# One layer of attention and experts: no long step in the second round, two adding transfers to a round

## The chip, the core and the metric

The kernel runs on one core of a Trainium2 chip. The core has five engines, each with a queue of its own that is worked off in order: TensorE (PE; its weight loads are listed apart as PEld), VectorE (DVE), ScalarE (ACT), GpSimd (POOL) and SyncE (SP, which issues DMAs). 16 DMA engines move data between the device's memory, called DRAM here, and the on-chip buffers. The metric is the device time of one execution in microseconds (us), lower is better.

## What is computed

The input x is [32, 256, 128] in float32: 32 sequences of 256 tokens with 128 features. Cut to what matters:

```python
xn = layernorm(x)
# attention: 16 heads of 8, rotary positions, a window of 64 tokens, causal
q, k, v = split(xn @ Wqkv.T); q, k = rotate(q), rotate(k)
a = softmax(where(allow, q @ k.T / sqrt(8), -inf)) @ v
attn = a @ Wproj.T + bproj
# experts: 8, of which each token takes 2
weights, indices = top_k(xn @ gate_w.T + gate_b, 2); weights = softmax(weights)
ffn = sum over e of w_e * (gelu(xn @ w1[e] + b1[e]) @ w2[e] + b2[e])
out = x + attn + ffn
```

## The kernel before

**Units of work.** Attention goes sequence by sequence (z = 0 to 31). Norms, projections and the tiles xs[u] (the input in SBUF, to which all results are added) go by pairs of sequences (u = 0 to 15). Routing goes by groups of 16 token tiles (g = 0 to 3, four u each).

**Rounds.** The order of the work on every engine is written out by hand. `Attention.run` goes through four rounds r for each sequence. A round emits the scores `sh` (L689, L701) of sequence z, of which DVE takes the maxima (L715), and the scores `sl` (L756, L770) of an earlier sequence, which ACT exponentiates (L780). `sh` has one buffer in PSUM, so the next round's `sh` can't begin before L715 is through. Besides, round 0 has the values of sequence z - 2 (L792, L801) and in odd z the sum of the rotated k (L618); round 1 the projection of the next pair (L596 on PE, L605 and L612 on DVE, then the rotation's product L611 on POOL); round 2 the second half of the values and the division (L801 to L827); round 3 in odd z the sum of the rotated q, then `parts` (L726 to L729) and `end` of sequence z - 2, which projects the attention's result and adds it into one half of xs[u] (L841, on DVE). `alone` (L627) copies the rotated k and q into the layouts km (in round 1, for the next sequence) and qm (in round 2) by four DMAs each on SP's queue.

**Beside the rounds.** At the end of each round `turn` takes one step of a second strand of work, `beside`, and then emits what was put off for POOL, among it L611:

```python
def turn(z, r):
    self.now = z, r
    next(beside, None)
    self.flush()
```

In this strand come, one after the other: norms and routing with the scatters; the experts; the collecting.

- *Norms and routing.* `norm` (L277) yields True before a long step (two tiles of L286 and L287 on DVE; the second one also has L289) and False before a light one (ACT's normalizing L303, PE's transposes L310 and gates L315, and so on). `route` (L326) does the same, with long steps on DVE of two to four instructions. In each round every strand that waits at a light step takes it; of long steps as many are taken as `room` says for that round (L1229).
- *Scatters.* Once a group is routed, its tokens are written to DRAM in the order of their experts (xs_d, L502), 128 indirect DMAs on POOL's queue, two to a round.
- *Experts.* When all scatters are issued, the loads of the first four blocks are issued, two more rounds pass, and then all 78 blocks of the experts are emitted in one round (L1011 to L1119). They write their results to ys_d in DRAM (L1087), one row for each token and choice.
- *Collecting.* `collect` (L1122) goes over the 16 u twice, for the first and the second choice (k = 0 and 1). One adding transfer (L1128, issued by POOL) reads 256 KB of ys_d and adds it to xs[u] in SBUF. After the second one of a u, those of its two sequences whose `end` is done are written to the output by `out` (L849, on SP's queue); the others are written by `end`. One transfer is issued to each `yield`, so to each round.

All accesses to xs[u] are kept in program order: `end` waits for an adding transfer into its xs[u] that was emitted before it, a transfer for an `end` before it, an output for both.

Of the kernel before, what the change touches and what calls it, by code (L numbers as in the profile page):

```python
# [105 lines left out]
def tile_layer(  # L106
# [87 lines left out]
    def loads_late():  # L194
        for u in range(3, NU):
            yield False
            load_x(u)
            if u == 3:
                nc.sync.dma_start(out=b1_n, in_=b1)
# [319 lines left out]
    class Attention:  # L519
# [327 lines left out]
        def out(self, z):  # L847
# [4 lines left out]
            )  # L852

        def run(self, beside):
            us = self.us
            first, stop = 2 * us[0], 2 * us[-1] + 2
# [15 lines left out]
# [4 lines that stand above are left out]
                self.past.clear()  # L876
# [245 lines left out]
    def collect():  # L1122

        for k in range(2):
            for u in range(NU):
                yield
                at = k * B * T + u * TB
                nc.gpsimd.dma_start(  # L1128
                    out=xs[u], in_=ys_d[at : at + TB, :].rearrange("(n p) d -> p n d", p=P),
                    accum_op=ALU.add,  # L1130
                )
                if k:
                    att.added.add(u)
                    for z in (2 * u, 2 * u + 1):
                        if z in att.ended:
                            att.out(z)

    def beside():
# [11 lines left out]
        def pack():  # L1150

            for e in range(NE):
                yield False
                nc.sync.dma_start(out=w_d[e, :, 0:H], in_=w1[e])
                nc.sync.dma_start(
                    out=w_d[e, :, H : H + NHC * D].rearrange("p (k d) -> p k d", d=D),
                    in_=w2[e].rearrange("(k p) d -> p k d", p=P),
                )
                yield False
                nc.sync.dma_start(  # L1160
                    out=w_d[e, :, H + NHC * D :], in_=b2_d[e : e + 1, :].to_broadcast([P, D])
                )

        def fills():

            yield False
            fill(0, NE)
            for e in range(NE):
                end = nc.sync.value_load(
                    ends[0:1, e : e + 1], min_val=ER * e, max_val=ER * (e + 1) - HT  # L1170
                )
                spread.append(
                    nc.sync.dma_start(
                        out=xs_d[bass.ds(end, HT), :], in_=void[:, e]
                    )
                )
                if e % 2:
                    yield False
# [21 lines left out]
        def begin(name, steps, urgent=False):  # L1200
            entry = [name, steps, next(steps)]
            going.insert(0, entry) if urgent else going.append(entry)

        def go_on(entry):
            entry[2] = next(entry[1], None)
            if entry[2] is None:
                finished.add(entry[0])
                going.remove(entry)
# [10 lines left out]
        u, g, last = 2, 0, False  # L1219
        while next(transfers, transfers) is not transfers:  # L1220
            z, r = att.now
            if (z, r) == (1, 0):
                begin("loads", loads_late())
            if (z, r) == (1, 1):
                begin("masks1", att.masks(1))
            if (z, r) == (3, 0):
                begin("pack", pack())

            room = ((2, 2, 0, 0) if z == 0 else (1, 1, 0, 1) if z % 2 else (2, 1, 0, 1))[r]  # L1229
            light = [e for e in going if e[2] is False]  # L1230
            for entry in light:
                go_on(entry)
            while room > 0:
                due = [e for e in going if e[2] is True and e not in light]
                if due:
                    go_on(due[0])
                elif u < NU:
                    begin(f"norm{u}", norm(u))
                    u += 1
                    continue  # L1240
                else:
                    break
                room -= 1
            if g < NG and all(f"norm{n}" in finished for n in range(NU // NG * (g + 1))):
                begin(f"route{g}", route(g, rt, misc), urgent=True)
                g += 1
            slots.extend(n for n in range(NG) if f"route{n}" in finished and n not in slots)
            if len(slots) == NG and not last:
                begin("blocks", blocks(rt, misc))
                last = True  # L1250
            if "blocks" in finished and "fills" not in [e[0] for e in going] + list(finished):
                begin("fills", fills())
            yield
# [3 lines left out]
        yield from experts()  # L1257
        apart(returned, "returned")
        yield from collect()

    att.run(beside())
    pools.close()

# [32 lines left out]
```

## Time and profile before

| | |
|---|---|
| median of 7 runs | 768.41 us (761.46 to 782.73) |
| the profiled execution | 757.22 us, span 755.4 us, granted TensorE clock 0.995 |
| busy: PE, DVE, POOL, ACT | 708.0, 494.7, 400.7, 385.2 us |
| L715, the maxima on DVE | 128 x 1220 ns |
| L780, the exponentials on ACT | 128 x 1023 ns |
| L502, scatters, on POOL | 128 x 993 ns |
| L1087, results of the experts, on POOL | 135 x 957 ns |
| from the start of L715 of round 1.0 to that of 22.3 | 29.09 to 350.28 us |
| round 22.3, with the experts | 350.28 to 616.85 us |
| rounds 23.0 to the end | 616.85 to 755.4 us |

A round z.r is round r of sequence z. The page of a profile gives the busy time of each engine over the span; "busy" doesn't say that an engine is what the others wait for. So the span is cut at the starts of L715, which comes once a round, and the windows between are compared with one another: a sequence with nothing beside it shows what attention alone takes. A timeline's row has start, duration, engine, line, tiles, count, and in brackets the idle time before it with what ended it.

### The profile page before, as it was taken

The numbers are of one execution on the slowest core, as the hardware profiler recorded it, in microseconds if no ns is written. First come the engines' busy times: TensorE is split into PE (matmuls) and PEld (weight loads), VectorE is DVE, ScalarE is ACT, GpSimd is POOL, SyncE is SP. The second block draws the span as 40 slices with busy tenths as digits, with TensorE's granted clock in tenths as the row PEclk, the third lists the DMA queues.
The fourth block names the chain that finished last, engine by engine and source line by source line (L and its number), as shares of the span: only waits on it lengthen the run. The fifth ranks groups of instructions, "written<-read, shape, count | busy, mean of one in ns | idle before, by whom it ended". The sixth has DMA issues, their size and how long they took to land.

```text
span 755.4 us, 20155 instructions
## 1 busy us (share of the span) xinstructions
PE 708.0 (94%) x7579; PEld 461.4 (61%) x7579; DVE 494.7 (65%) x1203; ACT 385.2 (51%) x727; POOL 400.7 (53%) x653
## 2 busy tenths in 40 slices
PE   7999999998999998998999999999999999999896
PEld 3445545444544444444999999899899964444342
DVE  5688998988998898786343343333333348787763
ACT  4666556556557454445444444344444454545452
POOL 2221068778788755782564555455555566363400
PEclk9999999999999999999999999999999999999999
DMA  3153442121121110225887887788788829589910
GB/s 107 53 168 86 127 135 71 45 68 53 47 70 46 57 56 26 81 75 174 257 250 242 254 258 234 242 242 245 228 257 251 252 58 125 90 128 186 190 45 16
DMA packets 86929, 105.67 MB, mean 140 GB/s; under 512 B 12824, under 2 KB 71352, under 8 KB 86832
## 3 DMA queue, kind: packets, MB, share of 16 engines
q1 hardware_dynamic: 61328, 78.59, 35.4%
q0 software_dynamic: 25312, 25.77, 15.6%
q8 instruction: 60, 0.98, 0.6%
q14 instruction: 37, 0.30, 0.1%
q10 hardware_dynamic: 192, 0.02, 0.0%
HBM read 73.51 MB, written 27.28 MB: 133 GB/s over the span
## 4 chain that ended last, share of the span: by engine, by line
PE 62%; DVE 15%; ACT 8%; DMA 6%; issue 5%; POOL 2%; SPq 0%; ACTq 0%; DVEq 0%; POOLq 0%
PE po L1074 13%; PE ph L1054 11%; PE sl L770 9%; PE sl L756 7%; ACT pr L780 7%; PE sh L701 6%; DVE mx L715 4%; PE y L792 4%; PE sh L689 4%; DMA ys_d<-yg,at 4%; DMA w<-w_d 2%; PE pm L739 2%; PE pg L315 1%; PE pxg L1039 1%; DVE yt L801 1%
## 5 line engine op out<-in xcount | busy, mean ns | idle before, releaser
L780 ACT ACTIVATE pr<-sl 128x1024 f32<-128x1024 f32 x128 | 130.9, 1023 | 175.4 <-PE sh L701 165.8
L1087 POOL DMA_INDIRECT ys_d<-yg,at x135 | 129.2, 957 | 129.6 <-DVE yg L1082 65.9
L715 DVE TENSOR_REDUCE mx<-sh 128x8 f32<-128x1024 f32 x128 | 156.1, 1220 | 56.6 <-PE sh L701 55.1
L1060 ACT ACTIVATE h<-ph,b_b 128x256 f32<-128x256 f32 (+1 forms) x312 | 117.6, 443 | 138.5 <-PE ph L1054 138.5
L502 POOL DMA_INDIRECT xs_d<-xn,slot x128 | 127.1, 993 | 33.7 <-issue 21.5
L701 PE MATMUL sh<-km,rq 32*64 32x512 f32 x1024 | 141.9, 614 | 2.1 <-ACT km L635 2.1
L770 PE MATMUL sl<-qm,rk 32*64 32x256 f32 (+1 forms) x1280 | 140.6, 480 | 0.0
L1074 PE MATMUL po<-w,h 128*128 128x128 f32 x1080 | 134.4, 276 | 4.9 <-DVE yg L1079 4.9
L1074 PEld LDWEIGHTS po<-w,h 128*128 128x128 f32 x1080 | 130.5, 192 | 10.9 <-DVE yg L1079 7.5
L1054 PE MATMUL ph<-xgT,w 128*128 128x256 f32 (+1 forms) x624 | 130.3, 352 | 1.4 <-ACT h L1060 1.2
L1054 PEld LDWEIGHTS ph<-xgT,w 128*128 128x128 f32 x624 | 102.6, 191 | 10.7 <-ACT h L1060 1.4
L756 PE MATMUL sl<-rs,pick_i 76*64 76x512 bf16 x512 | 79.7, 387 | 20.4 <-ACT pr L780 18.0
L1043 DVE COPY at<-xg 128x4 int32<-128x4 int32 (+1 forms) x78 | 14.8, 189 | 115.8 <-DMA ys_d<-yg,at 68.0
L770 PEld LDWEIGHTS sl<-qm,rk 32*64 32x64 f32 x1280 | 47.7, 130 | 38.8 <-issue 28.1
L792 PE MATMUL y<-pr,vst 128*32 128x128 f32 (+1 forms) x1536 | 68.9, 312 | 1.2 <-ACT pr L780 1.2
L792 PEld LDWEIGHTS y<-pr,vst 128*32 128x32 f32 x1536 | 39.4, 109 | 44.3 <-issue 37.2
L744 ACT COPY rs<-pm 12x1024 bf16<-12x1024 bf16 x63 | 60.2, 1001 | 9.6 <-PE pm L739 9.1
L1079 DVE TENSOR_TENSOR yg<-po,w 128x256 f32<-128x256 f32 (+1 forms) x78 | 30.3, 389 | 45.9 <-PE po L1074 43.9
L689 PE MATMUL sh<-mq,unit 64*64 64x512 bf16 x512 | 52.5, 399 | 4.9 <-DVE mx L715 4.4
L756 PEld LDWEIGHTS <-pick_i 76*64 76x64 bf16 x512 | 25.5, 107 | 51.3 <-issue 40.9
L801 DVE STREAM_TRANSPOSE yt<-y 128x512 f32<-128x512 f32 x64 | 45.3, 708 | 7.7 <-PE y L792 7.7
L689 PEld LDWEIGHTS <-unit 64*64 64x64 bf16 x512 | 15.9, 103 | 55.9 <-issue 55.1
(157 smaller groups left out, 840.7 us busy)
## 6 DMA issues: line engine op xcount, KB each, us to landing
w<-w_d SPq DMA_DIRECT2D x78, 576.0 KB
x<-ys_d POOLq DMA_DIRECT2D x32, 256.0 KB
xg<-xs_d SPq DMA_DIRECT2D x57, 130.0 KB
qm<-rq SPq DMA_DIRECT2D x128, 32.0 KB
w_d<-in_L_ffn_w_dram SPq DMA_DIRECT2D x16, 256.0 KB
out_dram<-x SPq DMA_DIRECT2D x32, 128.0 KB
km<-rk SPq DMA_DIRECT2D x124, 32.0 KB
x<-in_L_attn_x_dram SPq DMA_DIRECT2D x15, 256.0 KB
```

Source lines behind the costliest of these rows:

```text
L502: nc.gpsimd.indirect_dma_start(out=xs_d, out_offset=bass.IndirectOffsetOnAxis(ap=slot[:, n, k : k + 1], axis=0), in_=xns[n // NT][:, n % N ...
L689: nc.tensor.matmul(ps[HB * h : HB * h + HB, ii, :, :], lhsT=unit2[half, :], rhs=mq[half, which, :].unsqueeze(1).to_broadcast([HB, 4, 2 * HB]),
L701: nc.tensor.matmul(ps[HB * h : HB * h + HB, ii, :, :], lhsT=q[r, t * HB : (t + 1) * HB], rhs=km[r, :, t * HB : (t + 2) * HB], start=False, ...
L715: nc.vector.tensor_reduce(mx, ps, AX.X, ALU.max, negate=True)
L756: nc.tensor.matmul(ps[HB * e : HB * e + HB, ii, :, :], lhsT=pick_i[:, 2 * ip + ii, :], rhs=rs[e][:, :, n * P : (n + 1) * P], start=True, s ...
L770: nc.tensor.matmul(ps[HB * e : HB * e + HB, ii, :, lo:hi], lhsT=k[r, kt * HB : (kt + 1) * HB], rhs=qm[r, :, n * P + lo : n * P + hi], star ...
L780: nc.scalar.activation(pr, ps, AF.Exp, scale=1.0 / math.sqrt(HD))
L792: nc.tensor.matmul(py[32 * i : 32 * i + 32, 2 * o : 2 * o + 2, lo:hi], lhsT=self.vsts[z % 3][:, tile_, i, o, :], rhs=q["pr", n, i // 2][:, ...
L1054: nc.tensor.matmul(ph[:, j * BT : j * BT + t], lhsT=w[:, (k + j) * P : (k + j + 1) * P], rhs=xT, start=True, stop=True,)
L1060: nc.scalar.activation(h[:, k + j, :], ph[:, j * BT : j * BT + t], AF.Gelu, bias=b1_b[:, k + j, b : b + 1],)
L1074: nc.tensor.matmul(po[:, n, :], lhsT=h[:, k, n * P : (n + 1) * P], rhs=z[:, k, :], start=(k == 0), stop=(k == NHC - 1),)
L1087: nc.gpsimd.indirect_dma_start(out=ys_d, out_offset=bass.IndirectOffsetOnAxis(ap=at[:, n, 0:1], axis=0), in_=y[:, n, :], in_offset=None,)
```

## The change

Two edits. In `collect` the strand yields before every second transfer, so that two adding transfers are emitted to a round, 16 rounds instead of 32. In `beside` the number of long steps of the rounds 0 to 3 becomes 2, 0, 0, 1 in every sequence but the first (which keeps 2, 2, 0, 0), where it was 1, 1, 0, 1 in odd and 2, 1, 0, 1 in even sequences. What a step does, and the order of the steps among themselves, is as before.

```diff
@@ collect
         for k in range(2):
             for u in range(NU):
-                yield
+                if u % 2 == 0:
+                    yield
                 at = k * B * T + u * TB
                 nc.gpsimd.dma_start(
@@ beside
-            room = ((2, 2, 0, 0) if z == 0 else (1, 1, 0, 1) if z % 2 else (2, 1, 0, 1))[r]
+            room = ((2, 2, 0, 0) if z == 0 else (2, 0, 0, 1))[r]
```

With fewer long steps to a sequence the routing ends later: in the changed kernel the experts stand in round 25.3, before in 22.3.

## The prediction

> **What bounds the kernel now.** I read the page first, then the windows of each stage, then single rounds, then the queues of the adding transfers. I write z.r for round r of sequence z and cut time at the start of each round's L715 row on VectorE (DVE), of which there are 128. From the page:
>
> ```profile
> PE 708.0 (94%) x7579; PEld 461.4 (61%) x7579; DVE 494.7 (65%) x1203; ACT 385.2 (51%) x727; POOL 400.7 (53%) x653
> DMA  3153442121121110225887887788788829589910
> ```
>
> TensorE (PE) is the bound nearly everywhere, so only what stops it counts. The DMA row has two hills, the experts and, from slice 33, the adding transfers. The windows by stage (us, then busy time of PE, PEld, DVE, ACT, POOL, then clock, DMA share, GB/s):
>
> ```profile
> 45.46:281.95 236.49, 225.21 (x2924) 115.50 (x2926) 211.77 (x513) 138.75 (x227) 152.48 (x245) 1.00 0.26 78
> 281.95:350.28 68.33, 61.72 (x839) 29.06 (x828) 57.01 (x113) 31.93 (x43) 45.77 (x78) 1.00 0.22 68
> 350.28:616.85 266.57, 259.07 (x1883) 242.17 (x1886) 98.70 (x319) 121.90 (x319) 140.16 (x269) 1.00 0.78 238
> 616.85:655.89 39.04, 37.49 (x514) 17.42 (x510) 31.80 (x56) 20.04 (x27) 19.03 (x16) 1.00 0.70 103
> 655.89:708.24 52.35, 50.20 (x684) 23.36 (x680) 41.59 (x72) 26.72 (x36) 28.34 (x22) 1.00 0.95 154
> ```
>
> Norms and routing lie in the first two windows: DVE busy 212 of 236 us, almost as full as PE. The third is round 22.3, which holds all experts. The last two run at 13.09 us a sequence with nothing lost, although the transfers already take 0.95 of the DMA engines from 655.89 on. One free sequence, 24, by round:
>
> ```profile
> 629.71:633.09 3.38, 3.38 (x53) 1.73 (x46) 1.85 (x3) 2.94 (x3) 0.00 (x0) 1.00 1.22 171
> 633.09:636.42 3.33, 3.08 (x34) 0.91 (x38) 2.44 (x4) 1.06 (x2) 1.37 (x2) 1.00 0.03 8
> 636.42:639.59 3.17, 3.02 (x57) 1.40 (x50) 3.06 (x5) 0.98 (x1) 3.17 (x4) 1.00 0.46 58
> 639.59:642.80 3.21, 3.07 (x40) 1.80 (x43) 2.47 (x7) 1.70 (x4) 1.90 (x2) 1.00 1.23 150
> ```
>
> DVE has room in rounds 0 and 1 (1.85 and 2.44 us of 3.3) and none in round 2 (3.06 of 3.17). In odd sequences the sum L618 (0.68 us) takes room from rounds 0 and 3. GpSimd's (POOL's) timeline shows when transfers start:
>
> ```profile
> 619.27 2.75 POOL L1128 DMA_DIRECT2D x<-ys_d  x2 [1.60 <-DMA ys_d<-yg,at]
> 622.02 1.30 POOL L611 TENSOR_TENSOR rotq<-rotq,c 128x512 f32<-128x512 f32 x1
> 623.24 5.27 POOL L1128 DMA_DIRECT2D x<-ys_d  x4
> 635.05 1.26 POOL L611 TENSOR_TENSOR rotk<-rotk,c 128x512 f32<-128x512 f32 x1 [6.53 <-DVE rotk L605]
> 636.27 5.22 POOL L1128 DMA_DIRECT2D x<-ys_d  x4
> ```
>
> They come not one a round but in bursts of four, each let go by the rotation L611 of round 1. One costs POOL 1.3 us to issue. The burst of 636.27 is over by 645: that window, 638 to 645, moves 144 GB/s x 7 us = 1.0 MB, four transfers of 262 KB, at a DMA share of 1.17. So a transfer takes 1.8 us of full engines. With outputs beside it, it takes longer, which SyncE's (SP's) timeline shows:
>
> ```profile
> 675.07 2.11 SPq L849 DMA_DIRECT2D out_dram<-x  x1
> 677.28 3.12 SPq L627 DMA_DIRECT2D qm<-rq  x4
> 680.50 5.32 SPq L849 DMA_DIRECT2D out_dram<-x  x6
> 685.91 3.00 SPq L627 DMA_DIRECT2D km<-rk  x4
> ```
>
> Each pair of outputs waits for its transfer. In narrower windows the pairs start at 680.50, 682.57 and 684.80, so transfers land 2.15 us apart, and the copies km and qm stand behind them in SP's queue.
>
> **Part 1: no long step in round 1.** A long norm step is two tiles of L286 and L287 on DVE, 2 x (0.271 + 0.182) = 0.91 us; the second of a norm adds L289, 0.19. The order of instructions takes 16 such steps (norm or route) out of round 1 of sequences 1 to 17. Those rounds had a mean of 3.59 us against 3.33 without a step, so 17 x 0.26 = 4.5 us come free. All steps still have to be done. In eleven odd sequences round 0 now has two instead of one: L715 1.22 + L618 0.68 + L801 0.71 + 1.81 + 0.19 = 4.6 us of DVE where PE needs 3.4. Odd rounds 0 before (5, 7, 9, 11, 13) had a mean of 3.8, so the price lies between 0 (neighbours absorb it) and 11 x 0.8 = 8.8. Three more rounds 3 (18 to 20) carry a step; with one they took 4.07 against 3.21, so 2.6. POOL's scatters, PE's transposes and gates, and ACT's normalizing move with the steps, unchanged in number. Sum: -4.5 to +7. I take +2, since norms leave PE work of their own in the rounds that follow, which covers part. The planning steps (before in 18.1 to 18.3, 5.69 + 4.64 + 3.75 us) go to 21.1 to 21.3 at the same price.
>
> **Part 2: experts three sequences later.** With 3 steps a sequence instead of 3.5, the order of the changed kernel has route 3 done in 21.0 instead of 18.0, and the experts in 25.3 instead of 22.3. Their loads are still issued two rounds ahead of them. The block itself costs the same, 0. But only 24 rounds instead of 36 follow it.
>
> **Part 3: two transfers to a round.** I count t from the start of 26.0 and number transfers 0 to 31, 15 being the last of the first pass. From 616.85, the row in the same place before, the first issue is at t = 2.4, and data move from some 4.6 on (bytes of the queue). The order of POOL: four transfers, rotation 26.1, eight, rotation 27.1, eight, rotation 28.1, eight, rotation 29.1, four. Eight are 10.4 us of issue, against 14.4 us (8 x 1.8) of DMA at least, so POOL is ahead from then on and the engines never empty.
>
> Now a wait that before does not have. `end` (L841) of sequence 27 adds into the half tile xs[13] in round 29.3. Before it, in 29.2, transfer 29 (second pass, u = 13) is put in the queue, so DVE must wait for its landing. Undisturbed, L841 would come at 3 x 13.09 + 12.4 = 51.7 (12.4 from 629.27 - 616.85). Behind DVE stands L715 of 30.0, behind it PE, as `sh` has one buffer: the wait is paid in full, with 47.7 us of work to come (755.4 - 707.7, L841 of 27 standing like that of 29). Before, the last such wait was met: POOL ran ahead.
>
> Landing of 29: first 16 transfers, 4.6 + 16 x 1.8 = 33.4. Fourteen more with their outputs: at 2.15 us they land at 33.4 + 30.1 + 0.7 = 64.2. But the bursts of before left gaps into which outputs spilled, and here there are none. By bytes: 14 x 0.262 + 24 outputs x 0.131 + 0.6 MB of copies = 7.4 MB at 188 GB/s (window 704 to 716) is 39 us, landing at 73. Between 64.2 and 73 I take 67, nearer to the measured spacing: a wait of **15 us**. Ends: 8 (1.8 us throughout) and 21. Two smaller waits lie inside it and are not added: `end` of 25 in 27.3 needs transfer 12 (lands 28.5, wanted 25.5: 3 us); the km copies of 29 stand on SP behind outputs of transfers 16 and 17 (38) and land at some 44 where 41 + 3 is wanted.
>
> On POOL, the burst of four takes 5.22 us at a DVE that is busy 6.16 of 7 us: 1.3 each, as it is for a single one (649.42). The Trainium skill, page "SBUF — State Buffer", section "SBUF: two separate sides", warns that a DMA issued from GpSimd can starve, as its descriptors aren't written while VectorE holds the shared port. No such stretching shows in these rows; by that rule transfers would start later and the wait would only grow.
>
> **Sum.** On the profiled execution (757.22 us, span 755.4): +2 + 15 = 774. The median of the seven runs, 768.41, lies 1.5% above that execution, so I add the 17 to the median: **785 us**. Ends: 768.4 + 8 - 4.5 = 772, and 768.4 + 21 + 7 = 796.
>
> **Rivals.** (a) The transfers land in time and part 1 is a wash: -4.5 to +7, within 1%, some 769. It needs 30 landings in 51.7 - 4.6 = 47 us, 1.57 us each; no burst showed under 1.8 but for the mean of three at 656 to 663 (1.7). (b) Faster: the relief of round 1 counts in full and DVE's freed order also removes the idle of PE in the norm stage. From 45.46 to 350.28 PE idles 17.9 us, 13.0 of which free sequences show too (0.56 each); so -4.9 - 4.5 = -9, 759 us. It decides only if transfers also stay under 1.57 us. (c) Slower still: SP's order bites after the DVE wait too. km of 30 stands behind outputs of transfers 20 to 25; if transfers go at the 188 GB/s price (landing 73), the copies' own late landings of 29 and 30, 3 us each, come on top: 21 + 6 + 2, 797 us.
>
> **Chances.** Forecast 0.70, (c) 0.14, (a) 0.11, (b) 0.05. Within 1% (7.7 us, about what a measurement of this kernel can tell from no change) lies (a): same 0.11, faster 0.05, slower 0.84. The range 773 to 796 leaves out (b), most of (a) and the upper half of (c).
>
> **What would show it.** Right: a wait of DVE before L841 in round 29.3 for the transfer x<-ys_d, some 10 us or more; a DMA share over 1 without a gap from 5 to 60 us after the experts; a small wait in 27.3; the stretch from 26.0 to the end 8 to 21 us longer than from 23.0 before, less three sequences. Part 1: rounds 1 at 3.33, odd rounds 0 above 4. Wrong: sequences 26 to 30 at 13.09 us; or the stage before the experts longer or shorter than 7 us.

## The result and the profile after

The changed kernel takes 794.76 us (median of 20 runs, 783.53 to 805.43), the kernel before 768.44 us (48 runs on the same chip). The medians lie 26 us apart. The ratio, for which only the faster executions of either kernel count, is 1.0369, 95% interval 1.0336 to 1.0401: 28 us slower (768.41 us, on which the forecast was built, become 796.8), where 17 were forecast. The profiled execution of the changed kernel took 800.42 us, with a span of 798.6 us and a granted clock of 0.977. From its page, the busy times and, over 40 slices, the granted clock and the share of the DMA engines:

```profile
PE 726.3 (91%) x7579; PEld 466.2 (58%) x7579; DVE 498.7 (62%) x1203; ACT 385.1 (48%) x727; POOL 403.4 (51%) x653
...
PEclk9989999999999999999999999999999999997998
DMA  3152441111111112012177686877877676699910
```

The same 7579 matmuls took 18 us more. PEclk, the granted clock in tenths, is below 9 in slices 2, 36 and 39 (counted from 0, 20 us each). The last is the program's end: from round 31.3 on it takes 24.58 us, before 24.04. The other two lie at 40 to 60 and 719 to 739 us and hold two stalls that the kernel before does not have. Windows by stage (us, then busy time of PE, PEld, DVE, ACT, POOL, then granted clock, DMA share, GB/s); the first four are sequence 1, then from 2.0 to the experts, round 25.3 with the experts, and the first 38 us of what follows them:

```profile
29.49:51.24 21.75, 17.85 (x127) 7.52 (x127) 12.51 (x31) 10.77 (x22) 3.75 (x4) 0.79 0.39 112
51.24:402.41 351.17, 328.73 (x4261) 162.73 (x4260) 303.91 (x678) 190.01 (x295) 204.61 (x326) 0.99 0.22 66
402.41:684.71 282.30, 264.09 (x1883) 243.16 (x1886) 98.01 (x321) 121.90 (x318) 139.96 (x269) 0.99 0.73 226
684.71:723.00 38.29, 36.10 (x484) 16.88 (x477) 29.84 (x48) 19.43 (x25) 35.23 (x31) 1.00 1.22 160
723.00:735.00 12.00, 4.33 (x35) 1.46 (x37) 1.71 (x7) 0.84 (x4) 6.12 (x5) 0.72 1.39 197
735.00:751.21 16.21, 15.24 (x178) 6.71 (x174) 10.87 (x20) 6.56 (x10) 6.42 (x5) 0.89 1.04 203
```

Before, sequence 1 took 16.37 us. The window 723 to 735 is the second stall: TensorE is busy for 4.33 of 12 us while the share of the DMA engines is 1.39, and the granted clock is low in and behind it.

To compare stages I cut every trace at the starts of L715 and subtract 3.2725 us for each round, the price of a round with nothing beside it (13.09 / 4); what follows 26.0 is free at 99.5 us, as it was before (755.4 - 655.89). Chips differ in how fast they run either kernel, so a pair from a second chip stands beside the first one:

| us | before | after | before, other chip | after, other chip |
|---|---|---|---|---|
| start to 1.0 | 29.1 | 29.5 | 32.0 | 34.2 |
| sequence 1 | 16.4 | 21.8 | 16.1 | 22.5 |
| 2.0 to the experts, over the free price | 33.2 | 40.3 | 67.9 | 71.0 |
| the round with the experts | 266.6 | 282.3 | 277.6 | 283.8 |
| after the experts, over the free price | -0.2 | 14.4 | 0.5 | 17.3 |
| span | 755.4 | 798.6 | 804.5 | 839.1 |

Sequence 1, the rest of the norm stage and the stage after the experts make 5.4 + 7.1 + 14.6 = 27.1 us on the first chip and 6.4 + 3.1 + 16.8 = 26.3 us on the other, about the 28 of the ratio. That the two spans on the first chip lie 43 us apart, not 28, comes from the experts' round, 266.6 against 282.3 us: the profiled execution of before, at 757.22 us, was 11 us under its kernel's median, and the section on why the prediction was wrong comes back to this round.

**After the experts.** Lengths of single rounds in the trace of after: 26.0 to 27.2 between 3.17 and 3.38 us as in a free sequence, then 27.3 5.05, 28.3 **12.82**, 29.0 5.15 and 29.3 4.83, and free again from 30.0. GpSimd's timeline (start, duration, engine, line, tiles, count, and in brackets idle time and what ended it):

```profile
687.06 5.35 POOL L1129 DMA_DIRECT2D x<-ys_d  x4 [1.48 <-DMA ys_d<-yg,at]
...
704.19 11.65 POOL L1129 DMA_DIRECT2D x<-ys_d  x8
717.42 1.26 POOL L611 TENSOR_TENSOR rotk<-rotk,c 128x512 f32<-128x512 f32 x1 [1.57 <-DVE rotk L605]
718.63 10.49 POOL L1129 DMA_DIRECT2D x<-ys_d  x8
741.89 1.27 POOL L611 TENSOR_TENSOR rotq<-rotq,c 128x512 f32<-128x512 f32 x1 [12.77 <-DVE rotq L605]
743.12 5.20 POOL L1129 DMA_DIRECT2D x<-ys_d  x4
```

28 transfers go out in a stream. By the bytes of the queue they move without a gap from t = 4.3 (t counts from 26.0, 684.71) in some 48 us, 1.72 us each. The last four come late, since rotation 29.1 waits 12.77 us for a DVE that itself waits for a stalled TensorE. SyncE's timeline of the same stretch:

```profile
699.49 5.09 SPq L627 DMA_DIRECT2D km<-rk  x4
704.67 5.23 SPq L627 DMA_DIRECT2D qm<-rq  x4
718.13 2.70 SPq L849 DMA_DIRECT2D out_dram<-x  x4
720.93 6.05 SPq L627 DMA_DIRECT2D km<-rk  x4
727.08 5.56 SPq L849 DMA_DIRECT2D out_dram<-x  x4
```

After the copies of sequence 28 the queue does nothing from 709.9 to 718.13: its next entries are the outputs of the first two finished xs[u], which wait for transfers 16 and 17. Behind them stand the copies km of sequence 29. They are issued from 720.93 on, and TensorE wants them at 725. Who waits for it, from the view of waits after 684.7 (engine, tile, line and what ended the wait: total, times, longest):

```profile
PE sh L701 <- DMA km<-rk: 8.1, 2, 7.7
...
DVE x L841 <- DMA x<-ys_d: 3.3, 2, 1.7
```

TensorE waits 7.7 us for the copies, until 732.6, and its clock is at half for 10.2 us from 728.2 on. The wait that the forecast named, DVE's before L841, is there twice, at 712.22 and 750.87, but only 1.7 and 1.6 us long.

The semaphores in the trace tell when copies land. The four of sequence 28, issued from 699.49 on with no output near them, were in 10.5 us later, those of 29 after 11.7; four that were issued at 69.33, with no adding transfer running, took 3.6. With 3.6 us the copies of 29 would have been in at t = 39.8, just before they are wanted (an estimate). By this estimate the stall needs both: the place behind the outputs, and transfers that make the landing slow.

**Sequence 1.** Before, ACT exponentiates the scores `sl` of round 1.2 first and normalizes after it. The trace of before, ACT:

```profile
38.41 1.02 ACT L780 ACTIVATE pr<-sl 128x1024 f32<-128x1024 f32 x1 [3.73 <-PE sh L701]
40.29 0.88 ACT L303 ACTIVATE xn<-x,off,rstd 128x128 f32<-128x128 f32 x2 [0.85 <-DMA km<-rk]
```

After, ACT in the same place:

```profile
39.91 0.88 ACT L303 ACTIVATE xn<-x,off,rstd 128x128 f32<-128x128 f32 x2 [6.18 <-DVE off L296]
40.70 1.30 ACT L578 CAST rs<-c 64x256 bf16<-64x256 f32 x4
42.03 1.02 ACT L780 ACTIVATE pr<-sl 128x1024 f32<-128x1024 f32 x1
```

With two long steps in 1.0 the second half of that norm is done there, so its light steps, ACT's L303 first, are emitted at the end of 1.1, ahead of the exponentials of 1.2. ACT sits for 6.18 us behind the offset L296 of DVE, then does the norm and the copies L578, and comes to the exponentials at 42.03, 3.6 us later than before. TensorE needs them for its next scores (one row of its timeline in the trace of after):

```profile
43.10 1.06 PE L756 MATMUL sl<-rs,pick_i 76*64 76x512 bf16 x4 [3.80 <-ACT pr L780]
```

The same row before:

```profile
39.49 0.62 PE L756 MATMUL sl<-rs,pick_i 76*64 76x512 bf16 x4 [0.63 <-ACT pr L780]
```

Behind the longer wait the clock stands at half: the window 42 to 45 has 0.52 and 45 to 49 0.51, and the matmuls L701 take 1.11 us where they take 0.64 at the full clock. Round 1.2 takes 7.01 us instead of 2.86.

### The profile page after: what moved, and what is told of

Same layout as the page of the kernel before. It is cut to its first block, busy times and chain, and to the rows that moved or that the text cites. A ratio compares the mean times of both kernels' runs of the same rounds, so it can differ in the third digit from the quotient of the medians.

```text
span 798.6 us, 20151 instructions
## 1 busy us (share of the span) xinstructions
PE 726.3 (91%) x7579; PEld 466.2 (58%) x7579; DVE 498.7 (62%) x1203; ACT 385.1 (48%) x727; POOL 403.4 (51%) x653
## 3 DMA queue, kind: packets, MB, share of 16 engines
q0 software_dynamic: 25312, 25.77, 14.8%
## 4 chain that ended last, share of the span: by engine, by line
PE 43%; DVE 20%; DMA 16%; issue 7%; ACT 7%; POOL 4%; SPq 3%; DVEq 0%; ACTq 0%; POOLq 0%
DMA ys_d<-yg,at 9%; PE po L1074 8%; PE sl L770 7%; DVE mx L715 6%; PE sl L756 5%; PE ph L1054 5%; ACT pr L780 5%; PE sh L701 5%; DMA w<-w_d 4%; PE y L792 3%; PE sh L689 3%; POOL x L1129 2%; PE pg L315 2%; DVE yg L1079 2%; DVE yt L801 2%
## 5 line engine op out<-in xcount | busy, mean ns | idle before, releaser
L780 ACT ACTIVATE pr<-sl 128x1024 f32<-128x1024 f32 x128 | 130.9, 1023 | 193.7 <-PE sh L701 185.8
L715 DVE TENSOR_REDUCE mx<-sh 128x8 f32<-128x1024 f32 x128 | 156.2, 1220 | 72.6 <-PE sh L701 72.1
L701 PE MATMUL sh<-km,rq 32*64 32x512 f32 x1024 | 145.2, 627 | 10.2 <-DMA km<-rk 8.1
L1074 PE MATMUL po<-w,h 128*128 128x128 f32 x1080 | 136.5, 278 | 15.2 <-DVE yg L1079 14.7
L770 PE MATMUL sl<-qm,rk 32*64 32x256 f32 (+1 forms) x1280 | 146.5, 488 | 0.0
L1074 PEld LDWEIGHTS po<-w,h 128*128 128x128 f32 x1080 | 130.5, 193 | 25.1 <-DVE yg L1079 22.3
L792 PE MATMUL y<-pr,vst 128*32 128x128 f32 (+1 forms) x1536 | 71.5, 320 | 1.2 <-ACT pr L780 1.2
L744 ACT COPY rs<-pm 12x1024 bf16<-12x1024 bf16 x63 | 60.2, 1001 | 12.7 <-PE pm L739 12.5
```

Of the source, the lines that this page charges most:

```text
L701: nc.tensor.matmul(ps[HB * h : HB * h + HB, ii, :, :], lhsT=q[r, t * HB : (t + 1) * HB], rhs=km[r, :, t * HB : (t + 2) * HB], start=False, ...
L715: nc.vector.tensor_reduce(mx, ps, AX.X, ALU.max, negate=True)
L770: nc.tensor.matmul(ps[HB * e : HB * e + HB, ii, :, lo:hi], lhsT=k[r, kt * HB : (kt + 1) * HB], rhs=qm[r, :, n * P + lo : n * P + hi], star ...
L780: nc.scalar.activation(pr, ps, AF.Exp, scale=1.0 / math.sqrt(HD))
L792: nc.tensor.matmul(py[32 * i : 32 * i + 32, 2 * o : 2 * o + 2, lo:hi], lhsT=self.vsts[z % 3][:, tile_, i, o, :], rhs=q["pr", n, i // 2][:, ...
L1074: nc.tensor.matmul(po[:, n, :], lhsT=h[:, k, n * P : (n + 1) * P], rhs=z[:, k, :], start=(k == 0), stop=(k == NHC - 1),)
```

## The experiments

Ratios are against the kernel before on the same chip (it takes 816.53, 806.53 and 810.58 us as the median of the three sets of runs that gave intervals, the last two on one chip, and 821.8 us in one run on a further chip), with 95% intervals.

**The changed kernel again, and each edit alone.** First, on another chip, the changed kernel once more, then the edit of `collect` alone on the kernel before:

```diff
-                yield
+                if u % 2 == 0:
+                    yield
```

and the edit of `beside` alone:

```diff
-            room = ((2, 2, 0, 0) if z == 0 else (1, 1, 0, 1) if z % 2 else (2, 1, 0, 1))[r]
+            room = ((2, 2, 0, 0) if z == 0 else (2, 0, 0, 1))[r]
```

> The changed kernel once more, for a second profile. Its first one showed, against before: the stage from 1.0 to the experts about 13 us longer (5.5 of it in sequence 1), the experts 16 us longer, the rest from 26.0 on 114 instead of 99.5 us. Theory: sequence 1 (+5.5) and the rest (+14) come back, the experts' 16 us do not (they are 267 us within 4, as before), time 1.03 to 1.04 of before. Rival: the experts are longer because of the change and show 275 us or more again.

> Only two adding transfers to a round; long steps and the place of the experts (22.3) as before. Theory (a DVE add or a copy on SP waits for a landing that the pairs put too close ahead of it): transfer 28 (u = 12, second pass) now stands in 26.2, before the add of sequence 24 in 26.3, wanted 51.4 us after 23.0 and landing at 62 to 67, so 10 to 16 us more than before, ratio 1.013 to 1.021, and the stage ahead of the experts unchanged. Rival: only the late experts (24 rounds left instead of 36) make the transfers late: ratio 1.00 and 13.09 us a sequence after the experts.

> Only the long steps are moved (2, 0, 0, 1); one adding transfer to a round. Theory: from 1.0 to 25.3 the loss of the changed kernel comes in full: 8 to 13 us over before, 5 to 6 of it in sequence 1, where ScalarE takes two normalizings ahead of the exponential. Rival (as predicted): moving steps costs 2 us within -4.5 and 7. After the experts no wait for a landing up to the last rounds, but 24 rounds and 3 turns for 32 transfers: five are issued only at the end, some 8 to 12 us of tail. Ratio by the theory 1.022 to 1.033, by the rival 1.013 to 1.018.

Measured: the changed kernel 1.034 (1.0238 to 1.0442), after the experts +16.1 us. Its round with the experts took 282.7 us again, as the rival had it and not the theory. Pairs alone 1.0176 (1.0079 to 1.0273), after the experts +14.4 us, with the experts still in 22.3: round 25.3 took 14.38 us. From its view of waits after the experts:

```profile
PE sh L701 <- DMA km<-rk: 9.9, 2, 9.2
```

So the stall comes with the pairs, wherever the experts stand, and it is the same wait. Steps alone 1.0272 (1.0219 to 1.0324): sequence 1 takes 22.09 us, and after the experts it loses 13.1 us for another reason, as 24 rounds are too few for 32 single transfers: five stand behind all rounds in the program, and the last one waits for the last L841 (6.0 us of the 13.1 lie behind the start of 31.3; another 4.8 lie in 30.3, with a wait of 2.84 us for copies km). Neither edit is harmless by itself, and their prices don't add up: with pairs, the steps' tail is gone, so together they cost little more than the dearer one.

**Sequence 1 as before.** In the changed kernel, only its steps put back; and the reverse, only sequence 1 changed in the kernel before.

```diff
-            room = ((2, 2, 0, 0) if z == 0 else (2, 0, 0, 1))[r]
+            room = ((2, 2, 0, 0) if z == 0 else (1, 1, 0, 1) if z == 1 else (2, 0, 0, 1))[r]
```

```diff
-            room = (... else (1, 1, 0, 1) if z % 2 else (2, 1, 0, 1))[r]
+            room = (... else (2, 0, 0, 1) if z == 1 else (1, 1, 0, 1) if z % 2 else (2, 1, 0, 1))[r]
```

> The changed kernel, with the long steps of sequence 1 alone as before (1, 1, 0, 1). Theory: the wait of TensorE for the first exponential goes, and the lower clock behind it: 4 to 6 us less than the changed kernel, ratio to before 1.029 to 1.033. Rival: the 5.5 us of sequence 1 were a mishap of one execution, and the time is that of the changed kernel within 1 us.

> The kernel before with the long steps of sequence 1 alone as in the changed one (2, 0, 0, 1); experts stay in 22.3, one transfer to a round. Theory: ScalarE meets the two normalizings ahead of the exponential, TensorE waits 3 to 4 us and then runs at half clock for some us: sequence 1 takes 21.5 to 22.5 us instead of 16.5, ratio 1.006 to 1.009. Rival: the loss needs what follows in the later sequences too, and is taken up again: 1.000 to 1.003.

Measured: put back, sequence 1 takes 16.63 us instead of 22.40 on that chip, and the ratio goes from 1.034 to 1.027 (1.0199 to 1.0341; the two intervals overlap). Changed alone, it takes 22.03 us instead of 16.11, and the ratio is 1.0092 (1.0047 to 1.0138), 3.8 to 11.2 us of 810.58. That the new steps of sequence 1 cost some 6 us there is shown from both sides; that they do it through the order on ACT is read from the rows above, as no run changed that order alone.

**Which wait after the experts?** Theory: the copies km are late behind outputs on SP's queue. Rival, the forecast's: DVE must wait for a transfer before L841. One kernel holds back each output until 12 further transfers are issued, the last ones until all are (the edit in part):

```diff
+                    while len(late) > 12:
+                        put_out(late.pop(0))
...
-                    att.added.add(u)
-                    for z in (2 * u, 2 * u + 1):
-                        if z in att.ended:
-                            att.out(z)
+                    late.append(u)
```

Another leaves the outputs where they are and orders the transfers so that none is ahead of an `end` that comes soon (u = 14, 15 first, 12 and 13 last and one to a round); a third does both.

```diff
+        front = [14, 15, *range(12)]
+        order = [(k, u) for k in range(2) for u in front]
+        pairs = [order[n : n + 2] for n in range(0, len(order), 2)]
+        pairs += [[(0, 12)], [(0, 13)], [(1, 12)], [(1, 13)]]
```

> The changed kernel, but each output is put on SP's queue six rounds after its adding transfer instead of at once. Order of transfers and long steps as in the changed kernel. Theory now (SP holds the copies km of sequence 29 behind outputs, and the transfers then starve them): km of 29 is issued some 30 us after 26.0 instead of 36 and lands in time, so the 9.6 us wait ahead of 29.0 goes; DVE's add of 27 still waits for transfer 29, landing at 4.6 + 30 x 1.72 + 0.7 = 57 where 51.7 is wanted: 3 to 7 us left. From 26.0 to the end 103 to 107 us instead of 114 (free: 99.5). Rival (as predicted): the landing of transfer 29 sets the end alone, and moving the outputs only moves the wait to 29.3: 110 us or more.

> The changed kernel with the transfers in another order, so that no add of DVE has to wait for one (u = 14, 15 first, 13 after 29.3); outputs at once as in the changed kernel. Theory now: the km copies of 29 stand behind the same outputs and the wait ahead of 29.0 stays: from 26.0 to the end 109 to 114 us. Rival (as predicted): DVE's add of 27 was what held the end; 104 us or less.

> Both: transfers in the other order and outputs six rounds late; long steps as in the changed kernel. Theory now: nothing in the rounds waits for a landing or stands behind one: 99 to 103 us from 26.0 to the end; time 12 to 15 us under the changed kernel, ratio to before 1.013 to 1.02, which is what the long steps alone cost. Rival: transfers at two to a round starve the copies on SP's queue whatever their order, 106 us or more.

Measured after the experts: outputs late **+1.2** us, order alone **+9.5**, both **-0.3** (the changed kernel on this chip: +17.3). SyncE's timeline with the outputs late, counted from 26.0 at 721.9:

```profile
736.63 4.59 SPq L627 DMA_DIRECT2D km<-rk  x4
741.32 3.41 SPq L627 DMA_DIRECT2D qm<-rq  x4
744.83 4.15 SPq L627 DMA_DIRECT2D km<-rk  x4
```

The first row, the copies of 28, lies at t = 14.7, as in the changed kernel (14.8). The third, the copies of 29, lies at 22.9; in the changed kernel it was 36.2. So they could have gone 13 us before they did. The transfers run as hard as ever beside them (they have 113% of the DMA engines' time from 720 to 780), and still nobody waits for the copies. In the kernel with the order alone, where no L841 meets a transfer, the wait for the copies stays:

```profile
PE sh L701 <- DMA km<-rk: 4.4, 2, 4.1
```

That settles which wait it is. What is left with the outputs late, 1.2 us, is round 29.3 with 4.93 instead of 3.21: the forecast's wait before L841, 1.7 us long.

```profile
775.43 0.42 DVE L841 TENSOR_TENSOR x<-pj,x 128x256 f32<-128x256 f32 x1 [1.73 <-PE pm L739]
```

The row names PE's L739, but that stands behind this L841 in the program; the semaphore that DVE waits for here is that of transfer 29, which was in at 775.34. With the order moved as well, 29.3 takes 3.21. The totals are less clear than the stages: 1.0138 (1.0074 to 1.0202), 1.0313 (1.0251 to 1.0376) and 1.0246 (1.019 to 1.0301), and the third should not be above the first by its stages. Its four runs reach from 816.59 to 828.64 us and the profiled one was the fastest; the medians of all runs, 821.57 and 822.84 us, hardly differ. I trust the stages, and the difference of the two ratios stays unexplained.

**The copies on another queue.** In the changed kernel ACT issues the copies km from sequence 29 on.

```diff
-                        self.alone(z + 1, 1)
+                        self.alone(z + 1, 1, (nc.scalar,) if z >= 28 else (nc.sync,))
```

> The changed kernel, but the copies km of the sequences from 29 on are issued by ScalarE instead of SyncE; transfers, outputs and long steps as in the changed kernel. Theory (place in SP's queue): the copies no longer stand behind outputs, the wait of TensorE ahead of 29.0 goes, and what is left is DVE's waits for landings in 27.3 and 29.3 and a late qm: from 26.0 to the end 101 to 107 us. Rival (traffic): transfers and outputs at once fill the DMA engines so far that the copies land late whoever issues them: 110 us or more.

Measured: a single run, 847.17 us beside 821.8 for before, after the experts +17.1. Round 28.2 took 16.93 us. ACT's timeline:

```profile
769.66 5.25 ACTq L627 DMA_DIRECT2D km<-rk  x4
774.95 1.02 ACT L780 ACTIVATE pr<-sl 128x1024 f32<-128x1024 f32 x1 [14.35 <-DMA km<-rk]
```

ACT took up the copies only at 769.66, when SP's eight outputs had been issued (761.14 to 767.33), and held the exponentials for 14.35 us. In the trace each of the four copies waits for the semaphore of one of these outputs, so the kernel did not free them from the outputs. It can't separate a copy's place in the queue from the traffic beside it, and counts for neither.

**The pair on one chip, and all repairs at once.** Before and after were run again on one chip, together with a kernel that has the outputs late, the order moved and sequence 1 as before, but keeps the new steps from sequence 2 on.

> The kernel before, for a profile on the chip of the next three runs. Expected: 13.09 us a sequence from 23.0 on, sequence 1 at 16.4 to 16.6 us; the stage from 2.0 to the experts and the experts themselves as long as this chip makes them, to be taken from the others.

> The changed kernel for a profile on the same chip. Theory, stage by stage over before: sequence 1 +5.5 to 6; from 2.0 to the experts, over 3.27 us a round, +3 to +8 (three more sequences with long steps and more falls of the granted clock); experts 0 within 5; from 26.0 on +14 to 16. Rival as predicted for the stage ahead of the experts: +2 in all, sequence 1 included.

> Transfers in the other order, outputs late, and sequence 1 as before; from sequence 2 on the long steps of the changed kernel. What is left of the change is the long steps of the later sequences and the experts in 25.3. Theory: +3 to +8 us, ratio 1.004 to 1.010. Rival (part 1 as predicted, a gain in round 1 that is worth more than the price of the others): 0.994 to 1.002.

Measured: 806.32 and 840.93 us for the two (single runs; their stages are in the table above), and 1.0067 (1.0018 to 1.0116) for the repaired kernel: 5.4 us of 810.58. Its sequence 1 (16.09) and its stage after the experts (+1.0) are as good as before; what is left is the rest of the norm stage and the experts' round together.

**Another set of steps.** To that repair, two long steps in round 0 and one in round 1, none in round 3, which brings the experts to 25.0.

```diff
+            room = ((2, 2, 0, 0) if z == 0 else (1, 1, 0, 1) if z == 1 else (2, 1, 0, 0))[r]
```

> Transfers and outputs as in both, and other long steps: sequence 1 as before (1, 1, 0, 1), from sequence 2 on (2, 1, 0, 0), none in round 3, where DVE has no room. Experts in 25.0. Theory (a long step costs where DVE is full: 0.86 us in round 3, 0.26 in round 1): seventeen steps leave round 3, -14, eleven odd rounds 0 get a second one, +4 to +8, three more sequences with steps, +1 to +2, so the stage up to the experts is 4 to 8 us shorter than that of before; time 0.990 to 0.998 of before. Rival: what counts is DVE's sum and not the round, and the stage costs the same as in the changed kernel: 1.007 or more.

Measured: 1.0049 (0.999 to 1.0109), so the gain did not come, and no version was found that beats the kernel before. Its sequence 1 takes 20.31 us in spite of the old steps there: round 1.0 takes 8.35 us, as in the three traces taken with it (outputs late, order alone, both), which have the new steps. So that part is not due to the steps; its cause stays open.

## Why the prediction was wrong

**Part 1, the relief of round 1: right on the first chip.** There the 16 rounds 1 of sequences 2 to 17 went from 57.12 to 52.30 us, -4.8, where 4.5 was forecast for 17 of them. The eight odd rounds 0 among them rose by 0.9 us in all (0 to 8.8 was the range for eleven). On the other chip the rounds 1 gave only 1.5.

**Part 1, "POOL's scatters, PE's transposes and gates, and ACT's normalizing move with the steps, unchanged in number": this step failed.** Unchanged in number they were, but not in place on their engines' queues. In sequence 1 the moved light step puts ACT's L303 ahead of the exponentials L780, and that costs 5.4 to 6.4 us, which no term of the sum held. Later, rounds 2 of sequences 2 to 17 rose by 3.6 us, most of what rounds 1 gave, and the whole of these sixteen sequences came out at -0.5; that the cause is the same there is not shown. The rest of the norm stage's loss lies in the sequences that now have steps (18 to 20) or scatters (up to 25, where they ended in 22 before) for longer: on the first chip +4.1 in 18 to 22.2 and +3.1 in 23 and 24, with two rounds in part at half the clock (22.0 with 5.46, 24.0 with 4.39). On the other chip 2.0 to 22.2 came out 4.6 us shorter, and the loss, 7.7, lies wholly in the rounds from 22.3 to 25.2, which have scatters now and had none. I had priced that at 2.6 for three rounds 3. Part 1 was taken as +2, at most 7; with sequence 1 it is 9.5 to 12.5.

**Part 2: open within a few us.** The experts' round was costed at 0. Where it stands as before it took 266.6, 277.6, 277.6 and 286.2 us in four traces; in 25.3, 277.9 to 293.8 in ten. On the chip with the most traces it is 277.6 twice against a mean of 281.8 of five. The scatter of single runs is as wide as the difference. The repaired kernel bounds it: the experts and the rest of the norm stage cost 1.5 to 9.4 us together.

**Part 3: the size right by luck (+15 forecast, +14.4 measured), the wait wrong: this step failed too.** The forecast had two waits and put 15 us on DVE's before L841 in 29.3 and at most 3 us, hidden inside it, on the copies km of 29 behind the outputs. It is the other way round: with the copies out of the way, L841 waits 1.7 us. Two terms were mis-sized. The landing of transfer 29 was put at t = 67 by a spacing of 2.15 us or 188 GB/s for all; the transfers went at 1.72 us, with only eight outputs beside them up to t = 50 where the sum had 24, so that without a stall it lands at some t = 53 (L841 of 27 at 775.43 with the outputs late). And the copies, put at t = 44, landed at 47.9 where TensorE wanted them at 40.2: I had let them land 6 us after the outputs ahead of them (38 + 6); those came at 33.4, earlier than thought, but from the issue of the first copy, at 36.2, to the landing it took 11.7 us. That it landed at t = 66 in the changed kernel all the same (L841 of 27 at 750.87) is a consequence of the stall, since rotation 29.1 was late and the last four transfers with it, and no support for the forecast.

**What the copies' stall costs** is more than the wait. Round 28.3 lost 9.6 us, of which 7.7 are the wait and the rest is the half clock behind it; 29.0 lost 1.8 more. No term held the clock.

**The rivals.** Rival (c) named the mechanism, SP's order, and expected copies of 29 and 30 late by 3 us each on top of the DVE wait. On the other chip 28.3 lost 8.2 and 29.3 7.3 us, with waits of 6.3 and 5.3 us for copies km among them. The case was there and I gave it 0.14, because I priced it by the landing of a copy on a queue that was not crowded. Rival (a) asked for 30 landings at 1.57 us; they came at 1.72, close, and with 1.57 the copies would still have stood behind the outputs. Rival (b) fails with the rest of the norm stage: no idle of TensorE was won (22.4 us from 2.0 to the experts; before 17.9, and three free sequences would add 1.7).

**The sum.** Forecast +17; measured 28. The 11 us that are missing are, by the stages, mostly part 1's: sequence 1 with 5.4 to 6.4, the later sequences with 1 to 5 over what was taken.

## What to carry to other kernels

When work is moved between rounds, list for each in-order queue what now stands ahead of the operation that the bound engine waits for next: here a normalizing step ahead of the exponentials on ACT, and outputs that wait for their transfers ahead of ready copies on SP. A DMA that must wait belongs behind those that others need soon; holding back the outputs by a dozen transfers took 17.3 us of stall down to 1.2. Price a stall of TensorE with the slow clock that follows it.

## What the hardware showed

**The clock falls in fixed steps, and not only after a stall of TensorE.** In the profiled execution of before there is no fall between 32 and 751 us. After, between 32 and 793 us, the granted clock falls to 0.5 at 42.1 us (for 6.8), at 345.9, 376.6 and 444.9 (3.4 each) and at 728.2 (10.2): always a multiple of 3.4 us. The first and the last of these lie in the two stalls shown above. Beyond the wait of 7.7 us, rounds 28.3 and 29.0 lost 3.7 us. The Trainium skill, page "TensorE: Matmul & The Clock Gate", section "Part 1: The HAM clock gate (the "warmup" mystery)", says that an idle window of about 3.4 us halves the clock and that a busy one of the same length brings it back. The lengths agree with it. In the 3.4 us before the falls at 42.1 and 728.2 TensorE was busy for 0.64 and 0.19 us, as this rule has it; but before those at 345.9 and 376.6 it was busy for 2.63 and 2.12 us, and the clock fell all the same.

**Copies land late beside GpSimd's transfers.** While the adding transfers run without a gap, four copies of 32 KB take 5 to 6 us of SP's queue (3.4 to 6.4 with the outputs late) instead of 2.4, and land 8.4 to 11.7 us after the first was issued instead of 3.6. The skill's page "DMA: Bandwidth & Descriptors", section "SWDGE vs HWDGE vs iDMA", says that DMAs of GpSimd and those of SyncE feed different internal queues of a DMA engine, which takes turns between them. In the trace both move at once: in 4 us the transfers moved 0.70 MB alone (716 to 720), 0.66 MB beside copies (708 to 712) and 0.48 MB beside four outputs (720 to 724). So copies cost the transfers little, outputs some.

**Chips differ.** The kernel before takes 768, 807 to 811, 817 and 822 us on four chips. In the traces of the first and of one other chip most of the difference lies between 2.0 and the experts, where the scatters are (35 of 49 us before, 31 of 41 after; round 6.1 before: 3.23 us on the first chip, 4.90 on the other). Its cause was not looked into.
